# A four-layer GNN and FFN kernel: building the third layer's edge lists by one-hot products instead of scatters

## The chip, the cores and the metric

The kernel runs on one core of one Trainium2 chip. The metric is device time in microseconds (us) of one execution; lower is better. An engine executes its own queue in order: TensorE (PE, with its weight loads PEld), VectorE (DVE), ScalarE (ACT), GpSimd (POOL) and SyncE (SP, which here issues most DMAs). Where one engine needs another's result it waits on a semaphore.

## The reference

The input is 3125 nodes of 256 features and 50,000 edges, sorted by destination. Four layers follow each other, each a graph block and a feed-forward block. Cut to the blocks around the change:

```python
# second layer, graph block: dense normalised adjacency, two products
h = x @ W_pre + b_pre
h = relu(gcn_conv(h, W1, b1, src, dst, n))
h = relu(gcn_conv(h, W2, b2, src, dst, n))
y = h @ W_post + b_post
# second layer, feed-forward block: 8 experts, the best two of each node
...
# third layer, graph block: four sparse products
def spmm(h):
    return segment_sum(vals[:, None] * h[cols], rows, num_segments=3125)
h = x
for W, act in ((W0, relu), (W1, identity)):
    for _ in range(2):
        h = spmm(h) * 0.5
    h = act(h @ W)
```

In the third layer `rows` is `src` and `cols` is `dst`, so an edge adds its weight times the row of node `dst` to node `src`.

## The kernel before

Nodes are tiled as 25 tiles of 128 (`NT`), the last one partly empty. A graph product is mostly done as a dense product: the edges are scattered into tables in DRAM (`tw` for weights, `tcn` for counts), 128 edges at a time by indirect DMAs from POOL's queue (L645), and read back as tiles `tt` on SP's queue.

**The second layer's graph block** (`l1_gnn`, L1114) runs the function `spmm` (L252) twice over `tcn`: first with `h0`, then with `h1`. The features are split into a high and a low part in float32r (`h0` and `h0_lo`), so each step is two products. `spmm` takes destination chunks (`PARTS`: five of 512 columns, one of 384, one of 182); within one, for each of 25 source tiles `k` it issues four products (two halves of the features, two parts), 100 a chunk. Tiles come in DMAs of five `k`, with three buffers. When a chunk is complete, its follow-up is a generator whose steps are called between the next chunk's products: at every third `k`, in the last two chunks at every `k`. For the second product the follow-up is `second` (L1157): scale by `dinv` (L857, DVE), bias and relu (L1142, ACT), project (L364, PE), add to `x` (L236, DVE), then `front` of the second layer's experts: normalise (L1500 to L1520, DVE), transpose (L243, PE), router logits (L1573, PE), and on DVE the ranking of eight experts in about 30 small operations (L1281, L1287, L1541 to L1554). With the chunk that ends at tile 20, `front` also goes on to `plan_full` (L2186), which makes the first part of the experts' plan, on DVE with a few PE products (L2143 to L2164). The chunk after it is the second last.

**The lists.** The third layer's graph block does not use the dense table for nodes from tile 13 on (`NEAR`). Edges with such a `dst` are kept as lists: for each source tile, five columns (`EACH`) of 128 places, 125 columns (`SPOTS`) in all. A place holds three numbers: the row of `dst` to fetch, the place of `src` in its tile, and the weight. Unused places are zero. `load_lists` (L1265) reads the array `listed` from DRAM into `spots`; `l2_lists` (L1289) then fetches rows by indirect DMA (L1304), scales them (L1324, L1325), builds a one-hot matrix `one` (L1316) and multiplies.

`lists` (L1188) makes that array. The last 111 columns (`FARC`) of the edges, of 128 each, hold every edge that matters; `far_w` and `far_c` keep their weights and codes. DVE splits the code into `dst`, `src` and the source tile `home`, marks each edge's tile (`hot`), forms running counts over the columns (L1225, L1226) and over the partitions by PE products (L1235, L1236), and so has each edge's number `nth` within its tile. From this come a place and a column, and an address. Then a POOL loop of 111 indirect DMAs (L1253) stores 128 records of 12 bytes each at these addresses, with edges that don't count addressed beyond the end and dropped. `listed` was zeroed by a DMA from ACT's queue in `tables` (L566). All this works in one tile, `spare`, which `lists` cuts up by `carver` (L1172); `plan_full` later uses the same tile.

`lists` is a generator, but `l1_gnn` runs it through in one go between the two `spmm` calls (L1168). A scheduler then orders the instructions of each engine; it moves some of the list work behind products of the second `spmm`.

Of the kernel before, what the change touches and what calls it, by code (L numbers as in the profile page):

```python
# [10 lines left out]
F32 = mybir.dt.float32  # L11
F32R = mybir.dt.float32r
BF16 = mybir.dt.bfloat16
# [6 lines left out]
P = 128  # L20
# [48 lines left out]
class Net:  # L69
# [3 lines left out]
    def __init__(self, ctx: ExitStack, tc: tile.TileContext, ins, out):  # L73
# [39 lines left out]
        self.cond = self.dram.tile([2, D], F32, name="cond")  # L113
        self.listed = self.dram.tile([P * SPOTS, 3], F32, name="listed")
        self.far = [self.dram.tile([(NT - NEAR) * P, D], F32, name=f"far{r}") for r in range(4)]
# [135 lines left out]

    def spmm(self, table, h, stream, chunk, dt=F32, bufs=5, cold=False, lead=1, gate=None, dense=(), left=0):  # L252

# [11 lines left out]
        for some in [PARTS[:lead]] + [[c] for c in PARTS[lead:]]:  # L265
            cols = [slice(t0 * P, t0 * P + width(t0, nt)) for t0, nt in some]
            ps = [[self.psum()[:, : width(*c)] for _ in range(KD)] for c in some]
            for k0 in range(0, NT, kb):
# [10 lines left out]
                for j in range(kb):  # L279
                    k = k0 + j  # L280
                    for pair, tt in zip(ps, tts):
                        for m in range(KD):
                            for i, part in enumerate(h):
                                nc.tensor.matmul(  # L284
                                    pair[m],
                                    lhsT=part[:, k, m * P : (m + 1) * P],
                                    rhs=tt[:, j, :].bitcast(dt),
                                    start=k == 0 and i == 0,
                                    stop=k == NT - 1 and i == len(h) - 1,
                                )  # L290
                    if k % 3 == 2 or some[0][0] in dense:
                        next(steps, None)
            for _ in steps:
                pass
# [239 lines left out]
    def tables(self, pool, keep_w, keep, ordered, besides):  # L534
# [29 lines left out]
        nc.vector.memset(zero, 0.0)  # L564
        if ordered:
            nc.scalar.dma_start(self.listed.rearrange("(p c) v -> p (c v)", p=P), zero[:, 0, : 3 * SPOTS])  # L566
        eqs, cells, sums = {}, {}, []
# [546 lines left out]
    def l1_gnn(self, weights, after, last, ordered):  # L1114
# [3 lines left out]
        with self.reusing("l1g") as pool:  # L1118
# [38 lines left out]
            def second(t0, nt, ps):  # L1157
                fm = relu(t0, nt, ps, b2)
                yield
                for i in range(nt):  # L1160
                    self.add_to_x(t0 + i, self.project(fm, i, wo))
                yield from after(pool, t0, nt)

            dt = F32R if ordered else F32
            self.spmm(self.tcn, h0, pool, first, dt, 3, True, gate=lambda ld, n: self.gate(ordered, ld, "c", n))
            if ordered:
                self.spare = self.nm_tile("plan")
                for _ in self.lists(self.spare.rearrange("p t d -> p (t d)")):  # L1168
                    pass
            self.spmm(self.tcn, h1, pool, second, dt, 3, dense=(20, 23))  # L1170

    def carver(self, flat):  # L1172
        at = 0

        def tile_(shape, dt=F32):
            nonlocal at
            n = math.prod(shape)
            size = -(-n // 2) if dt == BF16 else n
            t = flat[:, at : at + size]
            at += size  # L1180
            assert at <= flat.shape[1]
            if dt != F32:
                t = t.bitcast(dt)[:, :n]
            return t.rearrange("p (a b) -> p a b", b=shape[1]) if len(shape) == 2 else t

        return tile_

    def lists(self, flat):  # L1188

# [4 lines left out]
        nc.vector.tensor_copy(one, self.ones)  # L1194
        rec, at, ok = tile_([n, 3]), tile_([n]), tile_([n])
        src, home, dst, i = tile_([n]), tile_([n]), tile_([n]), tile_([n], I32)
        nc.vector.tensor_scalar(i, self.far_c, 1.0 / NP, None, op0=ALU.mult)
# [9 lines left out]
        nc.vector.scalar_tensor_tensor(ok, dst, float(N), ok, op0=ALU.is_lt, op1=ALU.mult)  # L1207
        nc.vector.tensor_scalar(rec[:, :, 0], dst, -float(NEAR * P), None, op0=ALU.add)
        nc.vector.scalar_tensor_tensor(rec[:, :, 1], home, -float(P), src, op0=ALU.mult, op1=ALU.add)
        nc.vector.tensor_copy(rec[:, :, 2], self.far_w)  # L1210
        nc.vector.scalar_tensor_tensor(at, home, 1.0, ok, op0=ALU.add, op1=ALU.mult)
        hot = tile_([n, NT], BF16)
        nc.vector.tensor_tensor(
            hot,
            at[:, :, None].to_broadcast([P, n, NT]),
            self.iota[:, None, 1 : NT + 1].to_broadcast([P, n, NT]),
# [12 lines left out]
        step = 512 // NT  # L1229
        nth, part = tile_([n]), tile_([step, NT])  # L1230
        for c in range(0, n, step):
            m = min(step, n - c)
            flat = lambda t: t[:, c : c + m, :].rearrange("p c e -> p (c e)")
            ps = self.psum()[:, : m * NT]
            nc.tensor.matmul(ps, lhsT=tri, rhs=flat(hot), start=True, stop=False)  # L1235
            nc.tensor.matmul(ps, lhsT=one, rhs=flat(a), start=False, stop=True)  # L1236
            nc.vector.tensor_tensor(
# [6 lines left out]
        nc.vector.tensor_scalar(i, i, 7, None, op0=ALU.logical_shift_right)  # L1244
        nc.vector.tensor_copy(at, i)
        nc.vector.tensor_scalar(at, at, 1.0 - SPOTS * P, None, op0=ALU.mult)
        nc.vector.scalar_tensor_tensor(at, nth, float(SPOTS), at, op0=ALU.mult, op1=ALU.add)
        nc.vector.tensor_scalar(ok, ok, -float(2 * SPOTS * P), float(2 * SPOTS * P), op0=ALU.mult, op1=ALU.add)
        nc.vector.tensor_add(i, at, ok)  # L1249
        yield  # L1250
        done = []
        for c in range(n):
            st = nc.gpsimd.indirect_dma_start(  # L1253
                out=self.listed[:, :],
                out_offset=bass.IndirectOffsetOnAxis(ap=i[:, c : c + 1], axis=0),
                in_=rec[:, c, :],
                in_offset=None,
                bounds_check=SPOTS * P - 1,
                oob_is_err=False,
            )  # L1260
            for p in done:
                self.tc.declare_no_dep(st.ins, p.ins, reason="each edge has its own place")
            done.append(st)

    def load_lists(self, pool):  # L1265

        spots, spot_i = pool.tile([P, SPOTS, 3], F32, name="spots"), pool.tile([P, SPOTS], I32, name="spot_i")
        self.nc.sync.dma_start(spots, self.listed.rearrange("(p c) v -> p c v", p=P))
        self.nc.vector.tensor_copy(spot_i, spots[:, :, 0])
        self.spots = spots, spot_i  # L1270
# [18 lines left out]
    def l2_lists(self, h, loads, after, front):  # L1289
# [4 lines left out]
        with self.reusing("l2g", side="right") as pool:  # L1294
# [16 lines left out]
            def weigh(r, t):  # L1311
# [5 lines left out]
                    one,  # L1317
                    spots[:, s, 1:2].to_broadcast([P, EACH, P]),
                    self.iota[:, None, :].to_broadcast([P, EACH, P]),
                    op=ALU.is_equal,  # L1320
                )
                for j in range(EACH):
                    w = spots[:, t * EACH + j, 2:3]
                    nc.scalar.activation(hi[:, j, :], g[:, j, :], AF.Copy, scale=w)  # L1324
# [1102 lines left out]
```

## Time and profile before

| quantity | us |
|---|---|
| median of 18 runs (3385.61 to 3405.22) | 3396.73 |
| the profiled execution | 3396.24 |
| its span in the trace | 3393.9 |
| PE busy in the span | 3071.7 (91%) |
| DVE busy | 1651.5 (49%) |
| POOL busy | 1663.7 (49%) |
| ACT busy | 1016.5 (30%) |
| first product of the second layer (L284 with `h0`) | 865.7 to 1031 |
| second product (L284 with `h1`) | 1040.2 to 1238.6 |
| the 111 scatters of the lists (L1253) | 1061.0 to 1204.3 |
| the fetches of the third layer (L1304) | 1540.0 to 2250.2 |

A line of the timeline gives start, duration, engine, line and operation, output and inputs, shape, how many were merged, and in brackets the idle time before it with what ended it. A line of a group gives the total busy time, the mean in nanoseconds, and idle time before. A line of a stretch gives its bounds, its length, the busy time of PE, PEld, DVE, ACT and POOL with the number of instructions in brackets, the granted clock of PE as a fraction of full speed, the share of time in which the DMA engines were busy, and GB/s. A line of the waits gives who waited for whom, total us, how often, and the longest.

### The profile page before, as it was taken

How to read it: one execution, taken by the hardware profiler on the slowest of the kernel's cores; microseconds unless marked ns; L12 is line 12 of the kernel's file. 1: busy time of each engine (PE TensorE's matmuls, PEld its weight loads, DVE VectorE, ACT ScalarE, POOL GpSimd, SP SyncE). 2: the span in 40 equal slices, each digit the busy share in tenths (PEclk: the TensorE clock that was granted, in tenths of full speed). 3: DMA queues.
4: the chain of work that ended last, by engine and by line, in shares of the span. 5: the costliest groups of instructions: out<-in, count | busy, mean ns of one | idle time of the engine just before them, and what ended most of it. 6: DMA issues, size and time to landing. Idle time of an engine off the chain costs nothing. (4 is left out here: it accounts for less than half of the span.)

```text
span 3393.9 us, 48785 instructions
## 1 busy us (share of the span) xinstructions
PE 3071.7 (91%) x16878; PEld 2548.6 (75%) x16878; DVE 1651.5 (49%) x5227; ACT 1016.5 (30%) x2335; POOL 1663.7 (49%) x1633
## 2 busy tenths in 40 slices
PE   5677999997999969988989999998999969996997
PEld 4555888665787858877878898888999958885443
DVE  7994653668315455354444444676211154334233
ACT  4331000212211223423333333434444443222232
POOL 4777777777803724526777677633333300000332
PEclk8767999998999969998999999999999989998999
DMA  7987865001677839976767676654446567785440
GB/s 254 337 288 256 301 199 143 1 1 47 181 229 226 246 110 301 334 232 203 231 210 217 201 241 209 209 161 126 115 118 193 161 227 235 233 265 166 90 102 14
DMA packets 464108, 645.87 MB, mean 190 GB/s; under 512 B 75727, under 2 KB 314344, under 8 KB 463851
## 3 DMA queue, kind: packets, MB, share of 16 engines
q1 hardware_dynamic: 355500, 491.94, 44.7%
q0 software_dynamic: 75424, 113.17, 13.3%
q10 hardware_dynamic: 32926, 37.54, 3.4%
q8 instruction: 136, 2.23, 0.3%
q14 instruction: 122, 0.99, 0.1%
HBM read 605.36 MB, written 135.21 MB: 218 GB/s over the span
## 5 line engine op out<-in xcount | busy, mean ns | idle before, releaser
L1304 POOL DMA_INDIRECT got<-far,spot_i x500 | 500.4, 1001 | 250.2 <-issue 181.6
L284 PE MATMUL ps<-tt,h 128*128 128x512 f32 (+2 forms) x1400 | 525.6, 381 | 27.9 <-ACT h L337 24.0
L1422 PE MATMUL ps<-h,tt 128*128 128x256 f32 x1950 | 445.2, 380 | 5.0 <-ACT h L1350 3.5
L1422 PEld LDWEIGHTS ps<-h,tt 128*128 128x128 f32 x1950 | 360.9, 190 | 50.6 <-ACT h L1350 3.9
L2296 PE MATMUL ps<-xe,w 128*128 128x128 f32 x2688 | 325.7, 278 | 17.5 <-DVE rk L1287 7.1
L2296 PEld LDWEIGHTS ps<-xe,w 128*128 128x128 f32 x2688 | 320.1, 194 | 28.2 <-DVE rk L1287 7.3
L1324 ACT ACTIVATE hi<-got,spots 128x256 fp32r<-128x256 f32 x500 | 226.3, 500 | 354.4 <-PE ps L1396 195.0
L645 POOL DMA_INDIRECT tcn<-cnt,idx_c x285 | 287.1, 1007 | 86.9 <-issue 84.8
L284 PEld LDWEIGHTS ps<-tt,h 128*128 128x128 f32 x1400 | 270.7, 193 | 77.0 <-ACT h L337 24.8
L2305 PE MATMUL ps<-w,hid 128*128 128x256 f32 x1344 | 312.0, 382 | 0.0
L2313 POOL DMA_INDIRECT L_ffn_z<-yb,to x112 | 147.5, 1317 | 325.8 <-ACT hid L2299 177.1
L645 POOL DMA_INDIRECT tw<-tot,idx_w x273 | 264.4, 968 | 83.2 <-issue 80.8
L949 PE MATMUL ps<-hw,tt 128*128 128x256 f32 x1250 | 288.0, 389 | 14.1 <-DMA tt<-tw 9.3
L949 PEld LDWEIGHTS ps<-hw,tt 128*128 128x128 f32 x1250 | 240.2, 195 | 48.0 <-issue 10.0
L2299 ACT ACTIVATE hid<-ps,par 128x128 f32<-128x128 f32 x672 | 226.6, 364 | 151.3 <-PE ps L2296 118.0
L2305 PEld LDWEIGHTS ps<-w,hid 128*128 128x128 f32 x1344 | 248.2, 191 | 29.9 <-ACT hid L2299 0.4
L1325 DVE SCALAR_TENSOR_TENSOR lo<-got,spots,hi 128x256 fp32r<-128x256 f32 x500 | 216.8, 480 | 108.9 <-ACT hi L1324 107.6
L284 PE MATMUL ps<-tt,h_lo 128*128 128x512 f32 (+2 forms) x700 | 260.2, 376 | 0.0
L284 PE MATMUL ps<-tt,lo 128*128 128x512 f32 (+2 forms) x700 | 256.3, 373 | 0.0
L1253 POOL DMA_INDIRECT listed<-plan x111 | 109.7, 988 | 160.5 <-DVE plan L1249 127.0
L2250 POOL DMA_INDIRECT xb<-L_ffn_rows,of x112 | 109.5, 977 | 152.4 <-PE ps L2274 54.4
L597 DVE SCALAR_TENSOR_TENSOR eq<-cells,dinv_row,ahead 128x256 bf16<-128x256 f32 (+3 forms) x391 | 178.5, 514 | 0.3 <-ACT cells L584 0.3
(475 smaller groups left out, 4958.7 us busy)
## 6 DMA issues: line engine op xcount, KB each, us to landing
tt<-tcn SPq DMA_DIRECT2D x99, 1280.0 KB
w<-in_L_ffn_W SPq DMA_DIRECT2D x112, 1024.0 KB
tt<-tw SPq DMA_DIRECT2D x96, 640.0 KB
w<-in_L_ffn_W SPq DMA_DIRECT2D x112, 512.0 KB
tw<-zero_row SPq DMA_DIRECT2D x23, 1600.0 KB
tt<-tw SPq DMA_DIRECT2D x36, 768.0 KB
tt<-tcn SPq DMA_DIRECT2D x20, 960.0 KB
tcn<-zero_row SPq DMA_DIRECT2D x13, 1472.0 KB
```

The lines of the kernel that those rows point to most:

```text
L284: nc.tensor.matmul(pair[m], lhsT=part[:, k, m * P : (m + 1) * P], rhs=tt[:, j, :].bitcast(dt), start=k == 0 and i == 0, stop=k == NT - 1 a ...
L597: nc.vector.scalar_tensor_tensor(eqs[j], cells[k][:, at : at + m], self.col["w"][:, j : j + 1], ahead[:, GROUP * P - m :], op0=ALU.is_equa ...
L645: st = nc.gpsimd.indirect_dma_start(out=table[:, :], out_offset=bass.IndirectOffsetOnAxis(ap=idx[:, c : c + 1], axis=0), in_=src[:, c, :], ...
L949: nc.tensor.matmul(ps[:, i * D : (i + 1) * D], lhsT=tt[:, j - a, (i0 + i) * P : (i0 + i + 1) * P], rhs=hw[:, j, :], start=j == a, stop=j = ...
L1304: nc.gpsimd.indirect_dma_start(out=g[:, j, :], out_offset=None, in_=self.far[r][:, :], in_offset=bass.IndirectOffsetOnAxis(ap=spot_i[:, c ...
L1324: nc.scalar.activation(hi[:, j, :], g[:, j, :], AF.Copy, scale=w)
L1325: nc.vector.scalar_tensor_tensor(lo[:, j, :], g[:, j, :], w, hi[:, j, :].bitcast(F32), op0=ALU.mult, op1=ALU.subtract)
L1422: nc.tensor.matmul(ps, lhsT=tt[:, k, (t - t0) * P : (t - t0 + 1) * P], rhs=hs[r][:, k, :], start=k == 0, stop=False,)
L2296: nc.tensor.matmul(ps, lhsT=w1[:, k, h * P : (h + 1) * P], rhs=xe[:, k, :], start=k == 0, stop=k == KD - 1)
L2299: nc.scalar.activation(hid[:, h, :], ps, func, bias=par[:, h : h + 1])
L2305: nc.tensor.matmul(ps, lhsT=hid[:, h, :], rhs=w2[:, h, :], start=h == 0, stop=h == ht - 1)
L2313: st = nc.gpsimd.indirect_dma_start(out=z[:, :], out_offset=bass.IndirectOffsetOnAxis(ap=self.to[ph][:, 0, j : j + 1], axis=0), in_=yb, in ...
```

## The change

`lists` no longer scatters. Each edge's place `nth` (0 to 127) and column `home` (0 to 124, or beyond the end) are turned into one-hot rows: `place` (128 wide, float32r) and `which` (125 wide, bf16). For each of 111 edge columns, PE multiplies `place` (as weights) with `which` times the four values `dst`, `src`, and the weight's high part `tops` and low part `lows`, which is 500 columns wide; the sum over all edge columns is the array itself, with `tops` and `lows` added at the end. The work goes in 23 groups of five edge columns with two sets of buffers. A group is made in `made`: two comparisons on DVE, two multiplications on POOL, ten scaled copies on ACT. `summed` issues its products and adds the result from PSUM on DVE. The buffers lie in `spare` and in `h0_lo`, free after the first product.

`lists` is now passed to the second `spmm` as `side`, and one step is taken at every odd `k`. `second` runs what is left of it when it reaches the chunk before the plan's. The result is stored by one DMA on SP's queue, and `listed` has a new order: values outermost, so that `spots` is read as `[value, column]`.

```diff
@@ spmm @@
                     if k % 3 == 2 or some[0][0] in dense:
                         next(steps, None)
+                    if k % 2:
+                        next(side, None)
@@ tables @@
-        if ordered:
-            nc.scalar.dma_start(self.listed.rearrange("(p c) v -> p (c v)", p=P), zero[:, 0, : 3 * SPOTS])
@@ l1_gnn @@
             def second(t0, nt, ps):
                 fm = relu(t0, nt, ps, b2)
+                if t0 == NA:
+                    for _ in side:
+                        pass
                 yield
...
+            side = iter(())
             if ordered:
                 self.spare = self.nm_tile("plan")
-                for _ in self.lists(self.spare.rearrange("p t d -> p (t d)")):
-                    pass
-            self.spmm(self.tcn, h1, pool, second, dt, 3, dense=(20, 23))
+                side = self.lists(*(t.rearrange("p t d -> p (t d)") for t in (self.spare, h0[1])))
+            self.spmm(self.tcn, h1, pool, second, dt, 3, dense=(20, 23), side=side)
@@ lists @@
+        nc.scalar.copy(tops, self.far_w)
+        nc.vector.tensor_sub(lows, self.far_w, tops.bitcast(F32))
...
+        part_, some = self.carver(exact), 5
+        sets = [
+            (part_([some, P], F32R), tile_([some, SPOTS], BF16), part_([some, 4 * SPOTS], F32R)) for _ in range(2)
+        ]
+        sums = spots.rearrange("p v c -> p (v c)")
+
+        def made(c):
+            m = min(some, n - c)
+            place, which, vals = sets[c // some % 2]
+            wide = lambda t, k: t[:, c : c + m, None].to_broadcast([P, m, k])
+            for t, col, k in (which, home, SPOTS), (place, nth, P):
+                nc.vector.tensor_tensor(
+                    t[:, :m, :], wide(col, k), self.iota[:, None, :k].to_broadcast([P, m, k]), op=ALU.is_equal
+                )
+            for v, t in (0, dst), (1, src):
+                nc.gpsimd.tensor_mul(vals[:, :m, v * SPOTS : (v + 1) * SPOTS], which[:, :m, :], wide(t, SPOTS))
+            for j in range(m):
+                for v, t in (2, tops.bitcast(F32)), (3, lows):
+                    nc.scalar.activation(
+                        vals[:, j, v * SPOTS : (v + 1) * SPOTS], which[:, j, :], AF.Copy, scale=t[:, c + j : c + j + 1]
+                    )
+
+        def summed(c):
+            m = min(some, n - c)
+            place, which, vals = sets[c // some % 2]
+            ps = self.psum()[:, : 4 * SPOTS]
+            for j in range(m):
+                nc.tensor.matmul(ps, lhsT=place[:, j, :], rhs=vals[:, j, :], start=j == 0, stop=j == m - 1)
+            if c:
+                nc.vector.tensor_add(sums, sums, ps)
+            else:
+                nc.vector.tensor_copy(sums, ps)
+
+        made(0)
         yield
-        done = []
-        for c in range(n):
-            st = nc.gpsimd.indirect_dma_start(
-                out=self.listed[:, :],
-                out_offset=bass.IndirectOffsetOnAxis(ap=i[:, c : c + 1], axis=0),
-                in_=rec[:, c, :],
-                in_offset=None,
-                bounds_check=SPOTS * P - 1,
-                oob_is_err=False,
-            )
...
+        for c in range(0, n, some):
+            if c + some < n:
+                made(c + some)
+            summed(c)
+            yield
+        nc.vector.tensor_add(spots[:, 2, :], spots[:, 2, :], spots[:, 3, :])
+        nc.sync.dma_start(self.listed.rearrange("(v p) c -> p v c", p=P), spots[:, 0:3, :])
@@ load_lists @@
-        self.nc.sync.dma_start(spots, self.listed.rearrange("(p c) v -> p c v", p=P))
+        self.nc.sync.dma_start(spots, self.listed.rearrange("(v p) c -> p v c", p=P))
```

In the changed kernel's line numbers the comparisons are L1267, POOL's multiplications L1271, ACT's copies L1274, the list products L1283 and the sums L1285 and L1287. Lines of `spmm` up to its products keep their numbers; later ones are a few to 35 higher.

## The prediction

> **What bounds the kernel now.** I began with busy time by stretch. The scatters (L1253) run between 1061 and 1204 us, during the second sparse product of the third layer, so this stretch and its edges were read first. The page's own chain of waits names only the last store and is of no use here. PE, PEld, DVE, ACT and POOL busy time are followed by granted clock, DMA share and GB/s:
>
> ```profile
> 1040.20:1201.20 161.00, 160.47 (x817) 133.44 (x815) 85.61 (x391) 30.91 (x49) 107.22 (x109) 1.00 0.79 231
> ...
> 1205.00:1210.00 5.00, 2.04 (x14) 1.92 (x14) 3.29 (x12) 0.00 (x0) 0.00 (x0) 0.50 0.03 6
> ...
> 1230.00:1235.00 5.00, 5.00 (x25) 5.00 (x25) 0.49 (x3) 0.00 (x0) 0.00 (x0) 0.50 0.01 2
> ...
> 1700.00:1720.00 20.00, 14.66 (x72) 12.03 (x70) 9.52 (x21) 7.39 (x18) 15.43 (x16) 1.00 0.86 270
> ```
>
> From 1040 to 1201 PE is busy for 160.5 of 161 us at full clock: it is the bound. POOL's 107 us of scatters lie beside it and cost nothing there. Next the timeline, for PE's rate and for what the chunks add to it:
>
> ```profile
> 870.15 0.40 PE L284 MATMUL ps<-tt,h 128*128 128x512 f32 x1
> 870.39 0.39 PE L284 MATMUL ps<-tt,h_lo 128*128 128x512 f32 x1
> ...
> 1032.13 1.99 PE L364 MATMUL ps<-w,fmc 128*128 128x256 f32 x8 [0.76 <-ACT fmc L1142]
> 1038.12 2.47 PE L1235 MATMUL ps<-plan 128*128 128x500 bf16 x6 [3.99 <-DVE plan L1213]
> 1040.22 0.79 PE L284 MATMUL ps<-tt,h 128*128 128x512 f32 x1
> ...
> 1093.01 1.29 DVE L857 TENSOR_TENSOR fmc<-ps,dinv_row 128x512 f32<-128x512 f32 x2 [3.10 <-PE ps L284]
> ...
> 1121.06 1.29 DVE L857 TENSOR_TENSOR fmc<-ps,dinv_row 128x512 f32<-128x512 f32 x2 [3.07 <-PE ps L284]
> ```
>
> Products of 512 columns follow each other every 0.2333 us (three times that is 870.15 to 870.85). A chunk takes 1121.06 - 1093.01 = 28.05 us: 100 products are 23.33, and 4.73 go to projection, transposes and logits. At 1034.12 PE stops for 3.99 us because L1235 stands ahead of the second product. Last, what waits for the scatters:
>
> ```profile
> DVE plan L2143 <- DMA listed<-plan: 3.1, 1, 3.1
> ...
> PE ps L2164 <- DVE plan L2156: 7.7, 3, 6.8
> ```
>
> DVE waits 3.1 us for the scatters to land (the experts' plan reuses the buffer they read), inside a PE wait of 6.8 us that ends at 1207.96, after which the clock is 0.50.
>
> **The change, part by part.**
>
> *Removed.* 111 scatters leave POOL. In the stretch they cover PE was already full, so that is 0. The wait at 1203.6 goes: DVE's plan comes 3.1 us earlier and PE with it, -3.1. What is late next is the same plan work, 12 us of DVE operations. How much of the half-clock tail goes too the trace doesn't show. Bounds: 0, and all that PE has to spare between 1201.2 and 1244.3, 43 us for about 18 us of work at full clock (100 products of 182 columns, 0.11 apart there, and 7 us of others), so -25. I keep 0 beyond the 3.1, because 3.7 us of that PE wait stay, and a wait of 3.99 us (at 1034) also cost clock (0.75 in the next stretch). The zero fill of `listed` leaves ACT's queue at the start, where nobody waits for it: 0.
>
> *Moved.* The plan's first products (L1235) now come in the first chunk rather than ahead of it. PE starts the second product at 1034.1 rather than 1040.2 and runs the six products (2.1 us) later: -4.0. By instruction order the first of them stands after 72 chunk products, at 1034.1 + 16.8 = 1050.9; DVE's running sums for them end at 1050.5, so no new wait. The shorter pause gives about -0.5 of clock. A copy on ACT (`tops`, 0.285 by the 128x111 copy L486) now stands ahead of the activation that L364 waits for: +0.3. Sum -4.2.
>
> *Added on PE.* 111 products of 500 columns, float32r, each with its own weights like L284's: 0.2333 x 500/512 = 0.228, x111 = **+25.3 us**. PE is the bound there, and 0.5 us idle in 161 hides none of it.
>
> *Added on the engines that feed them.* For each of 23 groups of five edge columns DVE makes `which` and `place` (625 and 640 elements) and adds the last sums from PSUM; POOL multiplies twice (625 elements); ACT scales ten times (125 elements). The rows:
>
> ```profile
> L1148 POOL TENSOR_TENSOR x<-x,bo 128x1024 f32<-128x1024 f32 x5 | 11.7, 2377 | 0.0
> L1148 POOL TENSOR_TENSOR x<-x,bo 128x512 f32<-128x512 f32 x1 | 1.3, 1283 | 0.0
> ...
> L1316 DVE TENSOR_TENSOR one<-spots,iota 128x640 fp32r<-128x640 f32 x100 | 81.9, 820 | 150.1 <-PE ps L1396 149.1
> ...
> 1546.06 1.71 ACT L1324 ACTIVATE hi<-got,spots 128x256 fp32r<-128x256 f32 x4 [12.04 <-DMA got<-far,spot_i]
> ```
>
> POOL: between 512 and 1024 elements the slope is 1.094/512 = 2.14 ns, so 625 take 1.283 + 0.24 = 1.525 us; 44 of these and two of 125 (0.45 by the same line) are 68 us. DVE: L1316 is `place` in shape, 0.8; 44 and two short ones, 36 us. ACT: four of 256 in 1.71, a single one 0.51, so 0.40 apart; the casts L337 (256 in 0.396, 1024 in 1.052) slope at 0.85 ns, so 125 come 0.29 apart, and 222 are 64 us. Apart, each would fit beside PE. But POOL and DVE may not run together:
>
> ```profile
> 5.88 0.69 DVE L428 SCALAR_TENSOR_TENSOR rows_w<-rows_dst,rows_src 128x512 f32<-128x512 f32 x1
> 6.49 1.21 DVE L428 SCALAR_TENSOR_TENSOR rows_c<-rows_src,rows_dst 128x512 f32<-128x512 f32 x1
> ...
> 6.29 0.86 POOL L510 TENSOR_TENSOR crowd<-crowd,rows_src 128x256 f32<-128x256 f32 x1
> ...
> 919.27 14.79 POOL L1148 TENSOR_TENSOR x<-x,bo 128x1024 f32<-128x1024 f32 x7
> 923.03 11.58 DVE L336 TENSOR_SCALAR top<-whole 128x1024 int32<-128x1024 int32 x1 [5.94 <-ACT whole L1154]
> ```
>
> The same DVE operation with two SBUF inputs takes 0.69 us while POOL only writes, and 1.21 while POOL's two-input operation runs; taken from POOL's end at 7.15 it is 0.55 to 7.70. POOL's 0.86 for 256 elements is itself above the line (0.74). L336 (0.69 us elsewhere) waited until seven POOL operations in a row had ended, without getting in between. `which` and `place` have two SBUF inputs (`iota` and a column) and POOL's multiplications too, so I let them exclude each other: 68 + 36 = 104 us. Each group adds a hand-over from DVE to POOL (L1249 ends at 1060.76, the first scatter starts at 1061.03: 0.27), 6 us. In that time the router tails of two chunks pass DVE, some 30 small two-input operations and four normalizations each: 4.2 us a tail and 1.5 once, 10 us. Together 120.
>
> PE's own work beside it: DVE reaches the first group at 1072 (chunk 0 ends at 1059.5; from L857 to the last L1520 took 1064.95 to 1076.03, 11.1, and 1.5 for plan steps between), when PE is at its 136th chunk product; the last list product stands behind the 341st. So 205 x 0.2333 = 47.8, the lists' 25.3, and 1.3 + 4.7 + 3.5 of the three chunks touched: 82.6. PE takes its queue in order, so it waits for the rest: 120 - 82.6 = **+37.5 us**. Bounds: 0, if they do not exclude each other; and with POOL at its slowest row per element (L510, 0.865 for 256, so 2.1 for 625: 44 x 0.58 = 25 more) 63. I take 37.5, since L510 itself was waiting for DVE.
>
> A rule speaks here too: the Trainium skill, "SBUF — State Buffer", section "Who interferes with whom", says that a VectorE instruction with two SBUF inputs, or in a two-port mode, and a GpSimd one that reads SBUF block each other entirely, whatever their size. By it the small router operations count and the 10 us stay; by the row alone, which shows one scalar_tensor_tensor, they might not, and the wait would be 27.5.
>
> *Other queues moved past.* The store of the finished list stands in SP's queue between the fourth and fifth load of a chunk and waits for DVE's last sum. The fifth load is then issued some 2.5 us late, but is needed 40 products (9.3 us) after its usual issue and takes 1.3 MB at 231/0.79 = 292 GB/s, 4.5 us: 0, at most +2.5 with that cover gone. The lists are read back in runs of 500 bytes rather than 1500, the same 192 KB ahead of the first expert weights: 0 to +0.7, taken as 0. The fourth layer's reads of `spots` change their step only, on a DVE that is busy 9.5 of 20 us there: 0.
>
> *Sum.* 25.3 + 37.5 - 4.2 - 3.1 = +55.5. The profiled execution took 3396.24 us (span 3393.9), the median is 3396.73, so the two are interchangeable here: 3396.2 + 55.5 = **3452**.
>
> Will short pauses halve the clock? At 1700 us PE is busy for 14.66 of 20 us with clock 1.00, and 82.6 of 120 is a little less, so I add nothing. The Trainium skill, "TensorE: Matmul & The Clock Gate", Part 1, gives half rate after one idle window of about 3.4 us and full rate after as long a busy one. The stretch from 1230 disagrees with the second half, since PE is busy for 5.0 of 5 us at 0.50 there. By the first half the remaining 3.7 us wait still halves the clock and the end saves 3.1; by a recovery as quick as the rule's the tail would hold little more to win.
>
> **The rivals.**
>
> *PE alone decides (no exclusion).* ACT's 64 us and POOL's 68 are below 82.6, double buffers cover the rest: 3396.2 + 25.3 - 4.2 - 3.1 = 3414, to 3420 with some jitter. For it: only one operation in the trace shows the exclusion at one speed. Against: that one row is plain, and L336 too.
>
> *POOL is slower than its fp32 row, or the clock falls.* The multiplications read bf16 and a broadcast column, which no row shows. At 2.1 us the sum is 3396.2 + 55.5 + 25 = 3477; with PE at half clock 82.6 becomes up to 165, 45 above 120, so 3497. For it: PE would pause once a group, and longer at the router tails. Against: the stretch at 1700.
>
> *The end of the stage is cured: not slower.* One mechanism: the scatters' wait starts the half clock that lasts from 1205 to 1260, and without it the last chunk and its plan run at full clock. Price: up to -25 rather than -3.1, giving 3396.2 + 25.3 - 4.2 - 25 = 3392. It decides only if the feeding engines cost PE under about 4 us. For it: PE runs for 5 of 5 us at 0.50 from 1230. Against: DVE's plan chain of 12 us stays, and PE waits for it.
>
> That the change doesn't do what it says is excluded for the scatters: none are left in POOL's instruction order.
>
> **How the numbers follow.** Chances: forecast 0.63 (own range 3435 to 3475, POOL between 1.3 and 1.9 us and the 10 us of tails in or out), PE alone 0.22, slower POOL or clock 0.10, the end cured 0.05. The range holds the first two almost wholly and reaches into the third: 3409 to 3482. A measurement of this kernel tells about 0.2% (6.8 us) from no change. Faster by more than that lies only in the last case's edge, 0.02; within it 0.04; slower 0.94.
>
> **What would show it.** PE busy share in the stretch of the lists near 0.7 with waits of its list products (L1283) for POOL or ACT; POOL multiplications near 1.5 us each; DVE's `which` and `place` (L1267) well above 0.8 us on average, since their waits for the port count as their time; 111 list products 0.228 apart where fed; no 3.99 us wait at the second product's start; no DVE wait for the lists in the plan. The forecast is wrong if L1267 stays at 0.8 us while POOL multiplies (then 3414), if multiplications take 1 us or 2, or if the granted clock falls below 0.9 in that stretch.

## The result, and the profile after

The changed kernel takes 3430.56 us (median of 6 runs, 3428.49 to 3438.89), the kernel before 3395.54 us (37 runs). The ratio is 1.0112, 95% interval [1.0098, 1.0125], so the change costs 33 to 42 us. The forecast was 3452 with a range of 3409 to 3482.

The profiled execution took 3432.08 us (span 3430.3, before 3393.9: +36.4). To see where the time went, the stage of the change is cut at the starts of L857 (L859 in e8 and e12), the operation by which DVE takes a finished chunk out of PSUM: the *start* (last L857 of the first product to the first of the second), the *middle* (from there over four chunks, in which the lists are built) and the *end* (from there to the last L857 of the second product, with the experts' plan).

| us | start | middle | end | stage |
|---|---|---|---|---|
| before | 33.1 | 112.2 | 66.2 | 211.5 |
| after | 26.6 | 166.2 | 62.2 | 255.0 |
| difference | -6.5 | +54.0 | -4.1 | +43.4 |

Outside the stage the two profiles differ by -3.5 us ahead of it and -3.6 us behind it. Two later runs of variants on yet another chip had -2.0 and -0.7 (e11) and -0.8 and -8.4 (e12) there, so part of this at least is scatter between executions; whether any of it is the change's was not settled.

Busy time by stretch of the kernel after (PE, PEld, DVE, ACT, POOL with instruction counts, then granted clock, DMA share, GB/s):

```profile
1030.40:1056.20 25.80, 25.80 (x115) 20.27 (x114) 22.61 (x38) 1.93 (x4) 0.00 (x0) 1.00 0.82 278
...
1101.40:1160.70 59.30, 52.16 (x205) 39.67 (x206) 54.99 (x104) 44.65 (x143) 38.83 (x27) 0.85 0.34 113
...
1200.00:1220.00 20.00, 20.00 (x106) 16.16 (x106) 8.28 (x54) 3.82 (x7) 0.00 (x0) 1.00 0.69 211
...
1040.00:1201.00 161.00, 145.67 (x641) 113.11 (x640) 129.66 (x304) 85.76 (x255) 65.80 (x46) 0.93 0.52 167
```

PE was busy for 160.5 of 161 us over the last of these stretches, now for 145.7, and its clock is no longer full. In the chunk from 1101 DVE, not PE, is the fullest engine: 55.0 of 59.3 us. Behind the lists, from 1200, all is as before.

The timeline at the start of the second product, of the kernel after:

```profile
1028.67 1.99 PE L366 MATMUL ps<-w,fmc 128*128 128x256 f32 x8 [0.76 <-ACT fmc L1142]
...
1030.32 0.58 PE L284 MATMUL ps<-tt,h 128*128 128x512 f32 x1
```

The second product follows the first at once; the 3.99 us wait is gone. The waits in the plan (engine and tile, releaser, total us, times, longest), after:

```profile
PE ps L2198 <- DVE plan L2190: 4.1, 4, 3.0
```

Before, this wait was 7.7 us with 6.8 as its longest, and DVE waited 3.1 us for the scatters; that line is gone. What PE waits for while the lists are built:

```profile
PEld ps L1283 <- POOL h_lo L1271: 11.5, 7, 3.5
PEld ps L1283 <- ACT h_lo L1274: 9.2, 9, 4.1
PE ps L1283 <- ACT h_lo L1274: 6.5, 2, 3.7
PE ps L1283 <- POOL h_lo L1271: 3.8, 3, 2.6
PE ps L1283 <- DVE w L1583: 3.1, 1, 3.1
...
PE ps L1283 <- DVE rk L1321: 1.7, 2, 1.5
```

All are the list products (L1283), which wait for POOL, for ACT, and three times for DVE in its router work. Before the change PE waited for almost nothing here (PEld 0.7 us for ACT, PE 0.5 us for DVE). Part of the PEld waits lies under running products, so they are not added to the PE waits. Steady groups away from the router look like this:

```profile
1103.55 2.99 POOL L1271 TENSOR_TENSOR h_lo<-plan 128x625 fp32r<-128x625 bf16 x2 [0.97 <-DVE plan L1267]
1103.91 1.54 DVE L1267 TENSOR_TENSOR h_lo<-plan,iota 128x640 fp32r<-128x640 f32 x1
...
1105.37 1.83 DVE L1267 TENSOR_TENSOR plan<-plan,iota 128x625 bf16<-128x625 f32 x1
...
1107.34 3.00 POOL L1271 TENSOR_TENSOR h_lo<-plan 128x625 fp32r<-128x625 bf16 x2 [0.81 <-DVE plan L1267]
```

The first comparison begins during POOL's first multiplication and ends (1105.45) when the second is under way: it got in between the two, and the pair takes 2.99 us. The second comparison starts at 1105.37 but ends 0.7 us after the pair (1106.54), about its undisturbed length (0.80 at 1102.60), so it seems to have waited for the pair; and POOL starts again. A group takes 3.8 us of this chain; PE asks for one every 8 chunk products and 5 list products, 8 x 0.2333 + 1.14 = 3.0 us.

### The profile page after: what moved, and what is told of

Read it like the earlier page. It is cut to its first block, busy times and chain, and to the rows that moved or that the text cites. A ratio compares the mean times of both kernels' runs of the same rounds, so it can differ in the third digit from the quotient of the medians.

```text
span 3430.3 us, 49194 instructions
## 1 busy us (share of the span) xinstructions
PE 3107.1 (91%) x16989; PEld 2572.4 (75%) x16989; DVE 1723.2 (50%) x5296; ACT 1080.1 (31%) x2558; POOL 1620.2 (47%) x1568
## 5 line engine op out<-in xcount | busy, mean ns | idle before, releaser
L2330 PEld LDWEIGHTS ps<-xe,w 128*128 128x128 f32 x2688 | 318.7, 194 | 26.6 <-DVE cmp L1315 7.4
L1456 PE MATMUL ps<-n,tt 128*128 128x256 f32 x650 | 155.8, 396 | 17.9 <-DVE n L218 14.4
```

The costliest lines, as they stand in the source:

```text
L1456: nc.tensor.matmul(ps, lhsT=tt[:, k, (t - t0) * P : (t - t0 + 1) * P], rhs=hs[r][:, k, :], start=k == 0, stop=False,)
L2330: nc.tensor.matmul(ps, lhsT=w1[:, k, h * P : (h + 1) * P], rhs=xe[:, k, :], start=k == 0, stop=k == KD - 1)
```

## The experiments

Two remarks on how to read them. First, the runs e1 to e10 are of chips on which the kernel *before* takes 4094 to 4143 us, and e11 and e12 of one on which it takes 3392. The section on the hardware shows what is slow there: it is what runs beside scatters. The stage without scatters is not touched by it, as the changed kernel itself shows (e10: 254.3 us against 255.0), so runs are compared by the stage. Each stage is that of one profiled execution. e1, e3 and e4 leave work out, so their lists are not those of the reference and their total times tell nothing. Second, the expectations of e1 to e4 count the stage from the end of the last projection, 2.3 us less than from the last L857 (209.3 for 211.5); the table has the latter. *Excess* is the middle less 112.2 (before) + 25.3 (111 products of 0.228) + 2.1 (six products of the running counts, moved here) = 139.6, and for e12 less 112.2.

```
run                                start  middle   end   stage  excess
before                             33.1   112.2   66.2   211.5     -
after                              26.6   166.2   62.2   255.0   26.6
e10 after again                    26.5   165.7   62.1   254.3   26.1
e1  groups fed once                27.4   141.6   62.2   231.2    2.0
e2  a group every 16 products      26.5   163.7   61.7   251.9   24.1
e3  without POOL's products        26.6   146.5   62.3   235.4    6.9
e4  without ACT's scalings         26.5   168.8   61.8   257.2   29.2
e5  iota in PSUM                   26.5   159.6   62.2   248.3   20.0
e6  scalings on DVE, none on POOL  26.5   166.7   63.8   257.0   27.1
e7  scatters, own columns          33.1   248.1   62.1   343.3     -
e8  e7, interleaved                26.6   247.9   62.3   336.8     -
e9  quiet router, iota in PSUM     26.6   143.4   62.2   232.2    3.8
e11 quiet router                   27.9   148.5   61.9   238.3    8.9
e12 scatters, interleaved          26.6   112.8   70.2   209.6    0.6
```

### The products alone (e1), and the control (e10)

```
 def made(c):
     place, which, vals = sets[c // some % 2]
+    if c >= 2 * some:
+        return
```

> Leaves out the feeding of all groups but the first two: no comparisons, multiplications or scalings after them; the 111 list products and the sums stay and read the first two groups' operands again, so the lists are not those of the reference. The measure is the stage: from the end of the first product's last projection to the start of the last L857, 209.3 us before the change and 252.7 after it. It prices the products on PE alone. By the sum: 209.3 + 25.3 (products) - 4.0 (start) - 3.1 (scatters' wait) = 227.5 us, clock 1.00 up to the plan. If the products themselves cost more (their weights, their PSUM bank), the stage stays above 232.

Measured: 231.2 us, 228.9 by the expectation's measure. The middle is 29.4 us longer than before: 25.3 for the products, 2.1 for the counts, and 2.0, where the first group is waited for (2.65 us for POOL in the kernel after). The price of the products on PE is as forecast. The rest of the loss comes from feeding them.

> The changed kernel itself, as it is, as the control for the stages of the other runs, which are of chips on which the kernel before takes some 4140 us. If the stage has no part in that slowness once no scatters run in it, it is again 255 us (252 to 258) with an excess of 26.6 (23 to 30). If it is 262 or more, the stages of the other runs have to be read against this one.

Measured: 254.3 us, excess 26.1. On this chip the kernel before takes 4094 us and the changed one 4003.5: ratio 0.9777 [0.9730, 0.9824]. There the change is a gain.

### Which engine's feeding (e3, e4, e2)

```
-for v, t in (0, dst), (1, src):                    # e3, POOL
+for v, t in ((0, dst), (1, src)) if c < 2 * some else ():
-for j in range(m):                                 # e4, ACT
+for j in range(m if c < 2 * some else 0):
```

> Leaves out POOL's multiplications (destination and source columns) after the first two groups; comparisons, ACT's scalings, products and sums stay. Theory A (POOL against DVE): L1267 falls to 0.80 us throughout, and the stage to 235 us or less. Theory C (ACT, whose ten scalings a group stand in order behind the router's exponentials and stores): the waits for L1274 stay, stage 245 or more.

> Leaves out ACT's scalings (the weights' two halves) after the first two groups; comparisons, POOL's multiplications, products and sums stay. Theory A: the pairs of L1271 still take 3.0 us and a group 3.85 or more, L1267 still averages 1.1 us or more, stage 243 to 252 us. Theory C: the waits go with ACT, stage 235 or less.

Without POOL's multiplications the excess falls from 26.6 to 6.9 us, and L1267 to 0.81 us in the median. Without ACT's scalings it doesn't fall at all: 29.2, a stage of 257.2 us where theory A gave 243 to 252, and L1267 averages 1.08 us, a little under theory A's 1.1. So ACT is named in the waits, but it is POOL whose work costs the time: theory C falls. The router's work on DVE after a chunk, which is taken up below, took 25.6 and 18.8 us in this run.

```
     summed(c)
     yield
+    yield
```

> A group of five edge columns every 16 chunk products in place of every 8; nothing left out. Theory A (the feed of a group takes about 4.3 us, since POOL and DVE keep each other out, and PE waits in order only because it asks for a group every 3 us): PE now asks every 5 us, waits almost vanish, granted clock near 1.00, stage 227 to 233 us. Theory B (the feeding engines also disturb PE in some other way, or the tail of the plan is what grew): stage stays above 240.

Theory A as it stood here fell: 252.0 us. The waits of the list products almost went, and others came in their place. The waits of PE from the second chunk on in this run:

```profile
PEld ps L366 <- ACT fmc L1142: 13.9, 5, 4.5
PE ps L366 <- ACT fmc L1142: 11.8, 4, 4.1
PEld ps L1283 <- POOL h_lo L1271: 3.1, 1, 3.1
```

Now the *projection* (L366) of each finished chunk waits, and its releaser is ACT's activation, which is itself late. The timeline at a chunk's end says why:

```profile
1575.92 1.56 ACT L1274 ACTIVATE h_lo<-plan 128x125 fp32r<-128x125 bf16 x5 [4.72 <-DVE whole L1589]
...
1577.39 1.32 ACT L1142 ACTIVATE fmc<-fmc,col 128x512 f32<-128x512 f32 x2
1578.14 6.15 PEld L366 LDWEIGHTS ps<-w,fmc 128*128 128x128 f32 x16 [3.82 <-ACT fmc L1142]
```

ACT stood for 4.72 us at the previous chunk's router result (DVE's `whole`, L1589, which ACT's queue stores), then finished a group's scalings, and only then came to L1142. The router's tail on DVE, from the logits (`lg`) to the start of the last operation on `whole`, 39 small operations, took 5.4 us before:

```profile
1084.35 0.19 DVE L1585 TENSOR_TENSOR lg<-ps,br 128x32 f32<-128x32 f32 x1 [8.32 <-PE ps L1584]
...
1089.74 0.17 DVE L1554 TENSOR_TENSOR whole<-whole 128x4 f32<-128x4 f32 x1
```

In the kernel after it took 14.3 us, and 15.0 with the next chunk:

```profile
1085.66 0.18 DVE L1619 TENSOR_TENSOR lg<-ps,br 128x32 f32<-128x32 f32 x1
...
1100.00 0.75 DVE L1588 TENSOR_TENSOR whole<-whole 128x4 f32<-128x4 f32 x1
```

In e2 it took 14.5 us (1559.73 to 1574.26) and twice 12.1. Between the two lines of the kernel after stand eight DVE operations of the lists, five comparisons and three sums, whose durations add up to 8.1 us; those of the router's 39 add up to 8.8 us, for 6.9 before.

### The two places of the exclusion (e5, e6, e9, e11)

```
+iota = self.psum()[:, :P]
+nc.vector.tensor_copy(iota, self.iota)
...
-    t[:, :m, :], wide(col, k), self.iota[:, None, :k].to_broadcast([P, m, k]), op=ALU.is_equal
+    t[:, :m, :], wide(col, k), iota[:, None, :k].to_broadcast([P, m, k]), op=ALU.is_equal
```

> Nothing left out. For each group DVE first copies the iota into a PSUM tile (23 copies of 128x128, about 0.2 us each) and the two comparisons read it there, so they have one SBUF matrix input in place of two. The measure is the stage from the last L857 of the first product to the last L857 of the second: 211.6 us before the change, 255.0 after it, 231.1 with the groups fed once, 235.4 without POOL's multiplications. Theory A (POOL's multiplications and DVE operations with two SBUF inputs keep each other out): L1267 falls to about 0.8 us, the pairs of L1271 to 2.45, what is left of the exclusion is the router's small operations; stage 235 to 246, total ratio to before 1.005 to 1.008. If L1267 still takes 1.4 us and the pairs 3.0, the exclusion is of another kind (any DVE operation of this size, or the column operand alone), stage 250 or more.

Duration, min, median and max, of L1267 in the kernel after:

```profile
L1267 DVE TENSOR_TENSOR h_lo<-plan,iota x23: 279/1447/1896, 1066.8 to 1165.9; 128x640 fp32r<-128x640 f32 x22, 128x128 fp32r<-128x128 f32 x1
L1267 DVE TENSOR_TENSOR plan<-plan,iota x23: 775/808/1836, 1067.5 to 1164.7; 128x625 bf16<-128x625 f32 x22, 128x125 bf16<-128x125 f32 x1
```

And of the same comparisons (now L1269) and of POOL's multiplications (L1273) in e5:

```profile
L1269 DVE TENSOR_TENSOR plan<-plan,ps x23: 288/803/811, 1547.5 to 1636.5; 128x625 bf16<-128x625 f32 x22, 128x125 bf16<-128x125 f32 x1
L1269 DVE TENSOR_TENSOR h_lo<-plan,ps x23: 282/810/819, 1548.3 to 1636.7; 128x640 fp32r<-128x640 f32 x22, 128x128 fp32r<-128x128 f32 x1
...
L1273 POOL TENSOR_TENSOR h_lo<-plan x46: 396/1228/1256, 1548.7 to 1637.8; 128x625 fp32r<-128x625 bf16 x44, 128x125 fp32r<-128x125 bf16 x2
```

With one input in PSUM no comparison of 46 takes more than 0.82 us beside a busy POOL, and no multiplication more than 1.26 us; with both in SBUF they took up to 1.90 and 2.22. The exclusion is of two SBUF inputs on DVE against POOL's reading, as forecast. But the excess falls by only 6.6 us, to 20.0, short of what theory A expected. The router's small two-input operations still meet POOL: its tails take 15.6 us in e5, and 10.3 and 10.1 us in e3 where POOL is silent.

```
-nc.gpsimd.tensor_mul(vals[:, :m, v * SPOTS : (v + 1) * SPOTS], which[:, :m, :], wide(t, SPOTS))
+nc.vector.tensor_scalar(vals[:, j, v * SPOTS : (v + 1) * SPOTS], which[:, j, :],
+                        t[:, c + j : c + j + 1], None, op0=ALU.mult)
```

> Nothing left out. POOL's two multiplications a group become ten DVE operations of 125 elements with the column as a per-partition scalar (222 in all, by the 128x111 rows of L1197 to L1209 some 0.13 to 0.21 us each, 29 to 47 us of DVE). Theory A: without POOL no DVE operation waits for it, L1267 is 0.8 us, PE waits little, stage 234 to 242, ratio 1.003 to 1.007. If DVE's load as such delays the chunk's tail (L857 and the router behind it), stage 245 or more.

Measured: 257.0 us, no gain, the expectation's second case. L1267 is at 0.82 us, but DVE is now the bound; its busy time in a chunk of the lists (third value after the length):

```profile
1587.00:1645.00 58.00, 49.99 (x203) 36.79 (x203) 57.35 (x221) 42.11 (x130) 0.00 (x0) 0.85 0.37 123
```

DVE works 57.35 of 58 us. Its 222 operations take 0.218 us each of its time (48.3 / 222), so moving the work trades the exclusion for load.

The last two runs keep the feed but move it: from the second chunk on the lists' steps stand only among the first 14 of a chunk's 25 rows of products, ahead of the router's tail. e9 has the iota in PSUM as well.

```
-if k % 2:
+if k % 2 and (k < 14 or some[0][0] == 0):
     next(side, None)
```

> Nothing left out. As in the run with the iota in PSUM, and from the second chunk on the lists' steps stand only among the chunk's first 14 rows of products (7 steps a chunk), so POOL and the comparisons are quiet while the router's some 40 small DVE operations run in the last 11. The measure is the excess of the four chunk intervals from the first L857 of the second product on over 112.2 + 25.3 + 2.1 = 139.6 us: 26.6 after the change, 20.0 with the iota in PSUM, 24.1 with a group every 16 products, 6.9 without POOL's multiplications. Theory D (what is left is the router's tail and the feed in each other's way on DVE and ACT): excess 0 to 9 us, the small router operations back at 0.16 to 0.2 us, stage 231 to 238. If the excess stays above 15, the loss is one of the steady state (a group takes longer than its 8 chunk products and 5 list products on PE).

> Nothing left out. The lists' steps only among the first 14 rows of products of a chunk, as in the run with quiet in its name, but with the iota in SBUF, so the exclusion of POOL and the comparisons is back. Tells the two halves of that run apart. If the exclusion sets the steady state (a group takes 3.85 us of POOL and DVE against the 3.0 us after which PE asks for the next), 23 groups lose some 0.85 us each, less what two sets of buffers catch up in the quiet last 11 rows: excess 12 to 22 us. If the router's tail was nearly all of it, the excess is 4 to 9 us.

e9: excess 3.8 us, stage 232.2, ratio to before 0.9705 [0.9661, 0.9749] on its chip. The router's tails are 5.3 to 6.6 us again. Its busy time in a chunk with lists:

```profile
1540.00:1577.00 37.00, 36.57 (x177) 29.07 (x176) 29.30 (x91) 26.82 (x80) 16.88 (x14) 1.00 0.60 188
```

PE is full again, at full clock. e11: excess 8.9 us (the upper end of its second case), stage 238.3, so of the 26.6 us some 17.7 go with the place alone (it also spreads the groups over more time, seven steps a chunk for twelve, but e2 did that with the place kept, and gained 2.5), though L1267 still has medians of 1.31 and 1.36 us, and 5.1 more with the PSUM operand. e11 is also the check on time: 3416.83 us against 3391.66, ratio 1.0076 [1.0058, 1.0093], 25 us for a stage that is 26.7 longer.

### The start and the end, with the scatters kept (e7, e8, e12)

```
-tile_ = self.carver(flat)
+own_, tile_ = self.carver(flat[:, 5956:]), self.carver(flat[:, :5956])
...
-rec, at, ok = tile_([n, 3]), tile_([n]), tile_([n])
+rec, put, at, ok = own_([n, 3]), own_([n], I32), tile_([n]), tile_([n])
...
-tile_, hot = self.net.carver(flat[:, 3200:]), ...         # the experts' plan
+tile_, hot = self.net.carver(flat[:, 3200:5956]), ...
...
+if k % 2:                  # in spmm, e8 and e12 only
+    next(side, None)
```

> The kernel before, scatters kept; only the records and places that the scatters read lie in the last 444 columns of the buffer, which the experts' plan now leaves alone, so the plan no longer waits for the scatters. Prices the term -3.1 of the forecast, and the rival in which the scatters' wait starts the half clock at the end of the stage. By the forecast: stage 208.5 us, ratio 0.9991. By the rival: the granted clock from 1205 to 1250 rises above 0.8 and the stage falls to 190 to 200, ratio 0.994 to 0.997. If another wait takes its place: 211.6 and 1.000.

> The kernel before, scatters kept, records and places in their own columns as in the run with that name, and the lists' steps (running counts, their products, then the scatters) between the second product's chunk products as in the changed kernel. Prices the start: the second product no longer waits for the counts. By the forecast: stage 211.6 - 4.0 - 0.5 - 3.1 = 204, ratio 0.9978. The scatters start some 10 us later and end near the gather of the first expert's rows; if that gather is on the path, up to 4 us come back, ratio 0.999.

> The kernel before with the scatters kept, their records and places in columns of their own and the lists' steps between the second product's chunk products, again, for a ratio with a narrower interval and, should the chip be one on which the kernel before takes some 3396 us, for the time there: by the stages measured (start -6.6 + 2.1, end -4.1) 3396 - 8.6 = 3388, ratio 0.9975; on a chip with 4100 us for the kernel before 0.995 to 1.000.

In e7 and e8 the chunks beside the scatters are held up (see the section on the hardware), so their stages, 343.3 and 336.8 us, can't be held against the expected 208.5 and 204. The scatters end long before PE reaches the plan, so the plan waits for nothing: the end is 62.1 and 62.3 us, as in the kernel after, 4 us under the 66.2 of before. The clock over 39 us up to the last L857, in e7 and in the kernel before:

```profile
1812.00:1851.00 39.00, 28.66 (x169) 25.52 (x168) 22.32 (x116) 6.11 (x10) 3.87 (x4) 0.67 0.26 72
...
1204.00:1243.00 39.00, 27.75 (x163) 24.72 (x162) 19.38 (x103) 5.49 (x9) 4.13 (x5) 0.64 0.17 44
```

It is 0.67 for 0.64, far from the 0.8 of the rival. So the wait for the scatters was worth 4 us and was not what kept the clock low: the rival of the cured end falls. Whole-kernel ratios there: 0.9996 [0.9971, 1.0021] and 0.9972 [0.9945, 0.9999].

e12, on the chip of e11, shows both ends of the trade. The start is 26.6 us, as in the changed kernel. But the scatters now end later, and the wait comes back at another place in its end (70.2 us):

```profile
PE ps L366 <- ACT fmc L1144: 11.1, 1, 11.1
PE ps L243 <- DVE whole L1522: 9.6, 1, 9.6
...
DVE plan L2067 <- DMA listed<-plan: 7.2, 1, 7.2
```

The plan of the remaining tiles (L2067, a copy of the counts) writes the columns that the scatters read; DVE stands for 7.2 us, and the last chunk's router stands behind it. So the stage is 2.0 us shorter than before, not the 8.6 that was expected. The kernel takes 3386.65 us against 3391.66, ratio 0.9986 [0.9974, 0.9998]: of the three versions timed on chips like the first (the changed kernel, e11, e12) the only one that beats the kernel before, by 0.14% and just clear of the noise. Where the other 3 us of the 5 come from was not found. With the records in columns that this plan leaves alone too, the 7.2 us should go; that was not tried.

## Why the prediction was right, and where it was off

The sign and the range were right; the sum, +55.5 us, was too high by 12 us for the stage (+43.4) and by 21 us for the whole kernel (3430.56 for 3452). The time lies under the forecast's own 3435 to 3475 and over the 3420 of "PE alone", so neither case was hit as priced, and the range held because it spans both. (The prediction once calls the stretch of the scatters the third layer's second product; it is the second layer's.) By its terms:

- *Products on PE, +25.3.* Right: e1 finds 25.3 and 2.0 us of first waits.
- *Start, -4.2.* Right: -6.5 with the counts' 2.1 us moved behind it is -4.4.
- *End, -3.1.* Near: -4.1 (e7 -4.2). It was right not to credit the tail with more.
- *PE waits for the feeding engines, +37.5.* The step that was mis-sized: it measured 26.6. The forecast summed POOL and DVE as one locked resource to 120 us, took PE's own 82.6 us off, and let the clock stay full. The terms of that sum: POOL's multiplications were put at 1.525 us from its fp32 row and take 1.23 alone (e5: 53.8 us in all, not 68); the 2.99 us pairs, which look like the forecast's 1.5 each, have a comparison in them, so POOL's operations don't keep DVE out to the end of a run of them, as the row of L336 seemed to say. DVE's comparisons, 36 us, were right (e5: 18.1 + 17.9). The remaining 16 us, hand-overs and router tails, came in another way than the sum had it: the tails grew by 9 us each (14.3 and 15.0 us for 5.4), where the sum had put in 4.2 us a tail. In all the lists took 105 us, from 1066.8 (first L1267) to 1172.2 (last L1283).
- *The clock.* "I add nothing" was wrong. In the 24 windows of 5 us from 1060 to 1180 PE is idle for 15.3 us in all, and busy time times the missing share of the clock, an estimate of what the clock cost, is 8.9 us more. Together 24.3 of the 26.6. Stops of 2.65, 2.84, 3.15 and, around 1094.9 to 1101.6, of 1.48 and 3.67 us did this:

```profile
1100.00:1105.00 5.00, 3.35 (x6) 1.73 (x6) 5.00 (x8) 3.81 (x14) 4.03 (x4) 0.50 0.90 331
1105.00:1110.00 5.00, 4.32 (x10) 3.07 (x10) 5.00 (x5) 5.00 (x19) 4.19 (x3) 0.50 0.02 5
```

The prediction took the clock from a stretch of the kernel before, 1700 to 1720, with PE busy for 14.66 of 20 us at 1.00. But most of that idle time lies at its end, in stops of 1.46 and 3.53 us that begin at 1714.6 and 1716.8, and the clock falls in the next window:

```profile
1715.00:1720.00 5.00, 0.70 (x2) 0.30 (x2) 3.94 (x9) 2.91 (x8) 4.07 (x4) 1.00 0.52 155
1720.00:1725.00 5.00, 4.70 (x19) 4.36 (x20) 2.36 (x5) 1.77 (x4) 3.78 (x5) 0.66 0.32 84
```

So the idle time was over-estimated (15.3 us for 37.5) and the clock put at nothing from a stretch that was cut too soon (8.9 for 0); that the two errors partly cancel is luck.

The prediction's own signs say the same. Over the lists' whole stretch,

```profile
1066.80:1172.80 106.00, 90.67 (x379) 69.28 (x378) 93.61 (x183) 77.21 (x240) 65.80 (x46) 0.89 0.39 131
```

PE is busy for 0.86, not 0.7, and the clock is just under the 0.9 below which the forecast called itself wrong. L1267 averages 1.29 us, well above 0.8 as it should; the multiplications have a median of 1.24 us, not 1.5; the 3.99 us wait and DVE's wait for the lists are gone.

The account itself was right in kind and too simple in form. POOL and DVE do exclude each other, and the forecast's 10 us for router operations had the right place; but a sum over engines isn't what set the time: in e2 the same work has 151 us to be done in, and the excess is still 24.1. Moving the groups without removing any of the exclusion's work takes 17.7 of 26.6 us away (e11), because where the groups lay they held up the router's chain on DVE, with which ACT's and PE's queues wait in order. How much of the 9 us by which a tail grew is exclusion and how much mere queueing behind the lists' operations: with POOL silent a tail takes 10.2 us (e3; e6 the same) rather than 14.3 and 15.0, so about half each, an estimate. The Trainium skill, "SBUF — State Buffer", section "Who interferes with whom", has both halves of what the kernel after and e5 show (comparisons of up to 1.90 us against 0.82): a DVE operation with two SBUF inputs contends with a GpSimd operation that reads SBUF, and one with at most one such input, outside the two-port modes, doesn't.

The rival "PE alone decides" (3414) was wrong for this kernel, and is nearly what e9 reaches: stage +20.6 us, which on 3396 would be some 3416, an estimate, as e9 did not run on such a chip.

## What to carry to other kernels

Before work is put beside a full TensorE, look at the chain that already runs on the feeding engines: what a new group delays there (here a 5 us router tail that became 15) can cost more than the group's own engine time, and the wait shows up at another line. Place the new work where that chain is quiet, and give a VectorE operation that must run beside GpSimd one operand in PSUM. Where slowing the feed only moved the waits, as in e2, the place was at fault here and not the rate.

## What the runs showed of the hardware

*Scatters can hold up everything else, on some chips.* In e7, on a chip where the kernel before takes 4143 us, POOL issues its 111 scatters every 1.29 us as usual, and meanwhile nearly nothing else moves. Busy time by stretch of e7:

```profile
1560.00:1580.00 20.00, 4.46 (x8) 2.25 (x9) 0.00 (x0) 0.00 (x0) 15.13 (x17) 0.56 0.22 67
1580.00:1600.00 20.00, 0.58 (x1) 0.00 (x0) 0.00 (x0) 0.00 (x0) 15.42 (x16) 0.50 0.02 1
...
1705.00:1733.00 28.00, 28.00 (x143) 22.94 (x142) 12.08 (x64) 6.45 (x10) 0.00 (x0) 1.00 0.73 238
```

A chunk of 28 us takes 164. The DMA queues of the scatters' stretch, of e7 (1537 to 1680 us):

```profile
q1 hardware_dynamic: 2725, 5.42, 11.4%
q0 software_dynamic: 3520, 0.17, 2.3%
q8 instruction: 1, 0.02, 0.0%
q14 instruction: 2, 0.02, 0.0%
```

and of the kernel before on its own chip (1061 to 1204 us):

```profile
q1 hardware_dynamic: 17499, 31.20, 73.2%
q10 hardware_dynamic: 2636, 2.64, 7.8%
q0 software_dynamic: 3484, 0.17, 2.1%
q8 instruction: 6, 0.10, 0.3%
q14 instruction: 6, 0.05, 0.1%
```

A packet line gives packets, MB and share of time. The same 0.17 MB of scatters, but a sixth of q1's loads gets through beside them, and 3 packets of instructions for 12. That it is the scatters and not the chip alone is seen on the same chip: without them the stage takes 248.3 us in e5 and 257.0 in e6, with them 343.3 in e7 and 336.8 in e8. How the scatters hold up the rest no run shows. The three chips of e1 to e10 are of this kind, that of e11 and e12 and those of the first result are not; what makes a chip so was not found. It turns the sign of this change: ratio 0.9777 on the one kind, 1.0112 on the other.

*Short stops cost clock.* A stop of 2.65 us that ended at 1072.11 in the kernel after left the window from 1070 to 1075 at 0.66, and one of 3.15 us that ended at 1157.35 the window from 1155 at 0.70. After the stops of 1.48 and 3.67 us the granted clock stood at 0.50 for two windows in which PE was busy for 3.35 and 4.32 of 5 us, and at 0.74 in a third with PE busy throughout.
